# A norm's reciprocal root in two GpSimd steps, a divided output one round later, and nine shared SBUF buffers in a two-layer cross-attention kernel

## The chip, the cores and the metric

The kernel runs on one core of a Trainium2 chip. The engines are named as in the profile: PE is TensorE (PEld its weight loads), DVE is VectorE, ACT is ScalarE, POOL is GpSimd, and SP issues the DMAs. The metric is the device time of one execution in microseconds (us); smaller is better. The kernel before was timed in three runs: 3214.34, 3212.0 and 3215.55 us, with 3214.34 as their median.

## The reference

Two layers of the same block work on `x` of shape (4, 512, 320), with a context of shape (4, 1601, 192), all in float32. Each block has self attention with 20 heads of 16 columns, cross attention over the 1601 context rows, and a gated feed-forward part:

```
h1 = _ln(x, n1_g, n1_b)
x = _attn(h1, h1, q1, k1, v1, o1_w, o1_b, heads) + x
h2 = _ln(x, n2_g, n2_b)
x = _attn(h2, context, q2, k2, v2, o2_w, o2_b, heads) + x
h3 = _ln(x, n3_g, n3_b)
proj = h3 @ ff_w1 + ff_b1
a, g = jnp.split(proj, 2, axis=-1)
ff = a * jax.nn.gelu(g, approximate=False) @ ff_w2 + ff_b2
return ff + x
```

`_ln` subtracts a row's mean and multiplies by `rsqrt(v + EPS)`, then by a gain, and adds a bias. That reciprocal root is the first thing that the change touches. `_attn` takes a softmax over the keys.

## The kernel before, in words

**Units and chunks.** The program is a list of units that are emitted in order. A unit of attention is one batch row and one group of four heads, so there are 20 units of self attention and 20 of cross attention in each layer. A unit of the feed-forward part is one batch row. `main` works through a unit in chunks of 128 keys: 4 in a self unit, 13 in a cross unit. For each chunk PE computes the scores of four heads, keys along partitions, into PSUM tiles `st` (line 1062). ACT takes the exponentials into SBUF tiles `pr` (line 1068). One chunk later PE multiplies them with the values into a PSUM tile `av` (line 1082). PE also computes, among the scores, the scores `sps` of the next unit in the other orientation (line 891), from which DVE takes the row maxima (line 907).

**How `av` leaves PSUM.** The first chunk of a unit is copied by ACT to the unit's sum `o` (line 1093). Each later one is copied by ACT to a tile `vo` (line 1098) and added to `o` by GpSimd (line 1099). In the last unit of an attention stage DVE adds from PSUM instead (line 1095). `st` and `av` share one PSUM pool of four banks, so the scores of the next chunk need banks that ACT has read: those of the exponentials and that of `vo`.

**The pool `prs`.** The exponentials, the copied outputs `vo` and, in the feed-forward part, the gelu tiles `gl` share one SBUF pool with tag `pr` and eight buffers. When the four exponentials of a chunk are written, the four of the chunk before are still unread. That is eight. The fourth exponential of a chunk therefore gets the buffer that held `vo` of the chunk before, and ACT waits there for GpSimd's addition. In the program as built 574 exponentials carry such a wait for GpSimd, and no copy to `vo` does.

**The rest of GpSimd's queue.** Each engine runs its instructions in the order of the program. GpSimd also spreads projected queries and keys into slots of 32 rows (line 635: 0.48 to 0.56 us each by the profile's groups, eight for a self unit's queries and keys), adds a bias row to `x` (line 502), and takes the norm's root.

**The norm.** `add_norm` puts a norm's steps in a chain: statistics of four tiles of 128 rows (DVE, lines 464 and 465), `root`, the normalised rows `hn` (DVE, line 476), and transposes on PE (line 489). `root` calls `inverse_root`: three small DVE instructions make a first guess by integer arithmetic (lines 431 to 435), then one instruction scales and three Newton steps of four instructions each follow on GpSimd (lines 437 to 443), 13 in a row. `hn` may be emitted four rounds after `root`. A round is a tick of the planner's clock: a chunk of attention has two.

**The planner.** `steps` is called once a chunk, and runs pending pieces from the chains by their due times. `main` ticks the clock between the two halves of a chunk, and `steps` ticks it again. `LIGHT` pieces are limited to one or two a call. In `ff_main` the calls come at other intervals, and a pair of hidden blocks has four.

**A finished unit.** `add_finish` notes the round in `when`. `sums` (DVE transpose of `o`, line 979, and a reciprocal) may run two rounds later, then `divide`, then `turn`, whose four DMAs put the output into `aT`. The projections `ops` (line 1009) follow once five groups are there.

**The blank.** `blank`, a tile of 128 by 128, holds ones in the rows that carry the maximum and zeros elsewhere. DMAs copy it into the key buffers `kbuf` (line 138), whose last 128 columns begin at `4 * QT`.

Of the kernel before, what the change touches and what calls it, by code (L numbers as in the profile page):

```python
# [9 lines left out]
F32 = mybir.dt.float32  # L10
I32 = mybir.dt.int32
AF = mybir.ActivationFunctionType
ALU = mybir.AluOpType
# [9 lines left out]
P = 128  # L23
# [17 lines left out]
QT = (NC2 - 1) * 32  # L41
# [25 lines left out]
def kernel(ctx: ExitStack, tc: tile.TileContext, x, context, ws, out):  # L67
# [18 lines left out]
    nc = tc.nc  # L86
# [4 lines left out]
    one = ctx.enter_context(tc.tile_pool(name="one", bufs=1))  # L91
    two = ctx.enter_context(tc.tile_pool(name="two", bufs=2))
    three = ctx.enter_context(tc.tile_pool(name="three", bufs=3))
    prs = ctx.enter_context(tc.tile_pool(name="prs", bufs=8))
    dram = ctx.enter_context(tc.tile_pool(name="dram", bufs=1, space=bass.MemoryType.DRAM))
    ps_st = ctx.enter_context(tc.tile_pool(name="ps_st", bufs=4, space=PSUM))
    ps_m = ctx.enter_context(tc.tile_pool(name="ps_m", bufs=2, space=PSUM))
# [30 lines left out]
    nc.vector.memset(fill, 1.0)  # L128


    blank = const.tile([P, P], F32, name="blank")

    def blanks(k):

# [59 lines left out]
    def now(fs):  # L194
        for f in fs:
            f()
# [134 lines left out]
    LIGHT = 0.01  # L331
# [20 lines left out]
    def add(chain, cost, f, due, ready=yes, soon=yes):  # L352
        chains[chain].append((cost if isinstance(cost, tuple) else (cost,), due, ready, soon, f))
# [71 lines left out]
            assert chains[name], name  # L425
            run(name)

    def inverse_root(var):

        a, h, y, z = (two.tile([P, NQ], F32, tag=f"root{i}", name=f"root{i}") for i in range(4))  # L430
        nc.vector.tensor_scalar(a, var, EPS, None, ALU.add)  # L431
        nc.vector.tensor_scalar(
            z.bitcast(I32), a.bitcast(I32), 1, None, ALU.logical_shift_right
        )
        nc.vector.tensor_scalar(y.bitcast(I32), z.bitcast(I32), -1, 0x5F3759DF, ALU.mult, ALU.add)
        eng = nc.vector if start["on"] else nc.gpsimd
        eng.tensor_scalar(h, a, -0.5, None, ALU.mult)  # L437
        for _ in range(3):

            eng.tensor_tensor(z, y, y, ALU.mult)  # L440
            eng.tensor_tensor(z, z, h, ALU.mult)
            eng.tensor_scalar(z, z, 1.5, None, ALU.add)
            eng.tensor_tensor(y, y, z, ALU.mult)
        return y

    hn_used = []

# [7 lines left out]
    def add_norm(l, b, i, put, done, due):  # L455
        xb = xs[b]
        s = {}

        def stats(t):
            if t == 0:  # L460
                hn_used.append(b)
                s["mv"] = two.tile([P, NQ, 2], F32, tag="mv", name="mv")
            st = three.tile([P, 6], F32, tag="st6", name="st6")
            nc.vector.bn_stats(st, xb[:, t, :])
            nc.vector.bn_aggr(s["mv"][:, t, :], st)

        def root():
            s["rstd"] = inverse_root(s["mv"][:, :, 1])
            s["round"] = clock["round"]

        def normalise(t):
            if t == 0:
                s["hn"] = one.tile([P, NQ, D + REST], F32, tag="hn", name="hn")

            for to, at, n in ((0, 0, D), (D, D - REST, REST))[: 1 + i // 2]:
                nc.vector.tensor_scalar(  # L476
                    s["hn"][:, t, to : to + n], xb[:, t, at : at + n],
                    s["mv"][:, t, 0:1], s["rstd"][:, t : t + 1], ALU.subtract, ALU.mult,
                )
            s["round"] = clock["round"]  # L480

        def turn(k, at, n):
            if k == 0:
                s["hT"] = two.tile([P, 3, N], F32, tag="hT", name="hT")
                readers.append(done)
            ps = step_bank([P, N], "hps")
            n += REST if n == REST else 0
            for t in range(NQ):
                nc.tensor.transpose(ps[:n, t * P : (t + 1) * P], s["hn"][:, t, at : at + n], ident)  # L489
            if start["on"] and k == 1:  # L490
                nc.vector.tensor_scalar(
                    s["hT"][:n, k, :], ps[:n, :],
                    lng[i][:n, k : k + 1], lnb[i][:n, k : k + 1], ALU.mult, ALU.add,
                )
            else:
                nc.scalar.activation(
                    s["hT"][:n, k, :], ps[:n, :], AF.Identity,
                    bias=lnb[i][:n, k : k + 1], scale=lng[i][:n, k : k + 1],
                )
            for t in ((0,), (1,), (2, 3))[k]:  # L500

                nc.gpsimd.tensor_tensor(xb[:, t, :], xb[:, t, :], brow[(3 * l + i) % 2], ALU.add)  # L502
            if k == 2:
                hn_used.pop()
                put(s["hT"])

        for t in range(NQ):
            add(
                "norm", LIGHT, lambda t=t: stats(t), due - 22 + t,
                (lambda: stage[b] == 3 * l + i and not hn_used and b in loaded) if t == 0 else yes,  # L510
                (lambda: b == 0 or clock["round"] >= loaded[b] + 5) if t == 0 else yes,
            )
        add("norm", LIGHT, root, due - 18)
        for t in range(NQ):
            add(
                "norm", LIGHT, lambda t=t: normalise(t), due - 13 + t, yes,
                (lambda: clock["round"] >= s["round"] + 4) if t == 0 else yes,
            )
        for k, at, n in (DK if i < 2 else FK + [(2, 2 * P, REST)]):
            add(  # L520
                "norm", 0.58, lambda k=k, at=at, n=n: turn(k, at, n), due - 6 + 2 * k,
                may_overwrite if k == 0 else yes, lambda: clock["round"] >= s["round"] + 1,
            )
# [443 lines left out]
    def add_finish(u):  # L967

        when = [clock["round"]]

        def since(i, n):
            return lambda: len(when) > i and clock["round"] >= when[i] + n

        turned = two.tile([P, N // SLOT, SLOT], F32, tag="oturn", name="oturn")

        def sums():
            nc.vector.transpose(turned.rearrange("p b s -> p (b s)"), u.o)
            u.rd = two.tile([P, N // SLOT], F32, tag="rd", name="rd")  # L980
            nc.vector.reciprocal(u.rd, turned[:, :, DH])
            when.append(clock["round"])

        def divide():
            nc.vector.tensor_tensor(
                turned[:, :, :DH], turned[:, :, :DH],
                u.rd.rearrange("p (b o) -> p b o", o=1).to_broadcast([P, N // SLOT, DH]), ALU.mult,
            )
            nc.vector.transpose(u.o, turned.rearrange("p b s -> p (b s)"))
            when.append(clock["round"])  # L990

        def turn():

            if u.g == 0:
                held["outT"] = two.tile([P, 3, N], F32, tag="aT", name="aT")
            for j in range(HG):
                f = u.g * GD + j * DH
                k = next(k for k, at, n in DK if at <= f < at + n)
                row = f - DK[k][1]
                dma(out=held["outT"][row : row + DH, k, :], in_=u.o[j * SLOT : j * SLOT + DH, :])  # L1000
            if u.g == G - 1:
                end(held["outT"])

        def project(aT, t, part):
            cols = slice(part * D // 2, (part + 1) * D // 2)
            ps = step_bank([P, 512], "ops")
            for k, at, n in DK:
                for f, m in tiles_of(P):
                    nc.tensor.matmul(  # L1009
                        ps[f : f + m, : D // 2],  # L1010
                        lhsT=aT[:n, k, t * P + f : t * P + f + m],
                        rhs=wo[:n, k, cols],
                        start=(k == 0),
                        stop=(k == 2),
                    )
            nc.vector.tensor_tensor(xs[u.b][:, t, cols], ps[:, : D // 2], xs[u.b][:, t, cols], ALU.add)

        def end(aT):
            now = clock["round"]
            held["open"] += 1  # L1020
            for t in range(NQ):
                for part in range(2):
                    add(
                        "project", (0.317,) * 3, lambda t=t, part=part: project(aT, t, part),
                        now + 6 + u.nch * t + u.nch // 2 * part, yes, lambda: clock["round"] >= now + 3,
                    )
            add("project", 0.0, done, now + 6 + u.nch * NQ)

        def done():
            held["open"] -= 1  # L1030
            after(u)

        r = when[0]
        add("divide", LIGHT, sums, r - 20, yes, since(0, 2))
        add("divide", LIGHT, divide, r - 20, yes, since(1, 1))

        add("divide", 0.0, turn, r - 20, lambda: u.g or held["open"] < 2, since(2, 1))
# [325 lines left out]
    max_reduce(first)  # L1363
    max_end(first)
    now(load_x(1))
    now(blanks(kbuf[0][:, 4 * QT :]))
    loads.extend(load_x(2))
    for k in kbuf[1:]:
        loads.extend(blanks(k))
# [54 lines left out]
```

## Time and profile before

| what | value |
|---|---|
| runs | 3214.34, 3212.0, 3215.55 us; median 3214.34 us |
| the profiled execution | 3212.79 us, with a span of 3211.0 us and a mean granted TensorE clock of 0.999 |
| busy, share of the span | PE 99%, PEld 46%, DVE 64%, ACT 61%, POOL 37% |
| additions `o<-o,vo` on POOL (L1099) | 576, 736.2 us in all, 1278 ns each |
| exponentials on ACT (L1068) | 2720, 1412.7 us in all, 601 ns each |
| maxima on DVE (L907) | 974 and 339, about 1.2 us each |
| root on POOL (L437 and L440 to L443) | 23 roots of 13 instructions, 0.20 to 0.23 us each |

The span is the time from the first to the last recorded instruction. In a timeline a line begins with the start, in us from the span's start, and the duration in us; `xN` at the end means N instructions merged, and square brackets give the engine's idle time before the line and who ended it. A matmul of 32-bit numbers is recorded as two instructions, so one chunk's `av`, four matmuls, shows as x8.

### The profile page before, as it was taken

What the parts mean: (1) busy time and instruction counts of PE and PEld (TensorE: products, weight loads), DVE (VectorE), ACT (ScalarE), POOL (GpSimd) and SP (SyncE); (2) the same over time, 40 slices, a digit from 0 to 9 for tenths busy, and PEclk for the clock granted to TensorE, in tenths of its full rate; (3) what the DMA queues carried; (4) which work ended last, traced back from release to release, by engine and by line L of the source; (5) the groups of instructions that cost most, each with busy time, mean ns of one, the idle gap of its engine ahead of it and who ended that gap; (6) DMA issues with size and microseconds to landing.
All of it is one profiled execution on the core that took longest, in us unless ns stands there. A gap on an engine that the chain in (4) does not pass through costs nothing.

```text
span 3211.0 us, 81827 instructions
## 1 busy us (share of the span) xinstructions
PE 3170.7 (99%) x33970; PEld 1465.7 (46%) x33970; DVE 2062.9 (64%) x2663; ACT 1966.1 (61%) x3951; POOL 1203.1 (37%) x1617
## 2 busy tenths in 40 slices
PE   9999999999999999999999999999999999999999
PEld 3444444444444444354444444444444444443555
DVE  7776877778778677422247778777777777773221
ACT  4666577777777777611146665777778777785110
POOL 4555234444443443211225553344444444442000
PEclk9999999999999999999999999999999999999999
DMA  2130011100100100100012100010010010001000
GB/s 67 48 78 17 14 24 40 33 21 19 33 21 20 31 16 11 39 6 0 1 30 56 38 14 14 21 29 16 16 31 11 16 33 10 15 10 37 9 11 15
DMA packets 104999, 77.94 MB, mean 24 GB/s; under 512 B 42924, under 2 KB 95156, under 8 KB 104628
## 3 DMA queue, kind: packets, MB, share of 16 engines
q1 hardware_dynamic: 104544, 72.70, 9.3%
q8 instruction: 268, 4.39, 0.6%
q14 instruction: 103, 0.84, 0.1%
q0 software_dynamic: 64, 0.00, 0.0%
q10 hardware_dynamic: 20, 0.00, 0.0%
HBM read 33.04 MB, written 7.93 MB: 13 GB/s over the span
## 4 chain that ended last, share of the span: by engine, by line
PE 63%; DVE 2%; POOL 1%; ACT 0%; issue 0%; DMA 0%; SPq 0%; POOLq 0%; DVEq 0%
PE st L1062 15%; PE av L1082 13%; PE fps L1182 9%; PE sps L891 8%; PE yps L1221 5%; PE fps L1194 2%; PE ops L1009 2%; PE kps L743 2%; PE qps L687 2%; PE vps L836 2%; PE sps L915 1%; PE vps L818 1%; PE kps L713 1%; PE hps L489 1%; DVE nmax L907 1%; DVE pm L907 1%
## 5 line engine op out<-in xcount | busy, mean ns | idle before, releaser
L1068 ACT ACTIVATE pr<-st 128x512 f32<-128x512 f32 (+1 forms) x2720 | 1412.7, 601 | 432.1 <-PE sps L891 349.0
L1062 PE MATMUL st<-q,kT 32*128 32x512 f32 (+1 forms) x5440 | 1374.4, 615 | 9.7 <-ACT pr L1068 5.7
L907 DVE TENSOR_REDUCE pm<-sps 128x2 f32<-128x1024 f32 (+1 forms) x974 | 1134.8, 1203 | 271.9 <-PE sps L891 265.8
L891 PE MATMUL sps<-kT,q 32*128 32x512 f32 x5120 | 1272.6, 620 | 14.3 <-DVE nmax L907 11.7
L1099 POOL TENSOR_TENSOR o<-o,vo 128x512 f32<-128x512 f32 x576 | 736.2, 1278 | 1389.0 <-ACT vo L1098 1248.3
L1062 PEld LDWEIGHTS st<-q,kT 32*128 32x128 f32 (+1 forms) x5440 | 511.3, 181 | 528.0 <-ACT pr L1068 309.3
L1082 PE MATMUL av<-pr,vals 128*32 128x512 f32 (+1 forms) x5440 | 730.4, 605 | 0.2
L907 DVE TENSOR_REDUCE nmax<-sps 128x2 f32<-128x1024 f32 (+1 forms) x339 | 378.4, 1157 | 155.9 <-PE sps L891 152.8
L891 PEld LDWEIGHTS sps<-kT,q 32*128 32x128 f32 x5120 | 408.5, 183 | 120.7 <-issue 79.3
L1098 ACT COPY vo<-av 128x512 f32<-128x512 f32 x576 | 347.4, 603 | 41.8 <-PE av L1082 37.8
L1082 PEld LDWEIGHTS av<-pr,vals 128*32 128x32 f32 (+1 forms) x5440 | 109.9, 108 | 495.3 <-ACT pr L1068 483.5
L1182 PE MATMUL fps<-hT,w 128*128 128x512 f32 x640 | 288.2, 599 | 1.1 <-DVE hid L1201 0.6
L1200 ACT ACTIVATE gl<-fps,b 128x512 f32<-128x512 f32 x80 | 50.7, 684 | 387.4 <-PE fps L1194 387.3
L635 POOL TENSOR_SCALAR q<-qst,keep,zero 64x128 f32<-64x128 f32 (+1 forms) x476 | 230.4, 484 | 48.6 <-ACT qst L699 15.4
L1182 PEld LDWEIGHTS fps<-hT,w 128*128 128x128 f32 x640 | 117.3, 190 | 148.6 <-issue 143.2
L1201 DVE SCALAR_TENSOR_TENSOR hid<-fps,b,gl 128x512 f32<-128x512 f32 x48 | 33.8, 746 | 163.1 <-ACT gl L1200 163.1
L1009 PEld LDWEIGHTS ops<-wo,aT 112*32 112x32 f32 (+1 forms) x3072 | 97.7, 110 | 68.4 <-issue 37.6
L687 PE MATMUL qps<-hT,wq 112*32 112x128 f32 (+3 forms) x2880 | 125.6, 308 | 0.5 <-DVE pm L907 0.5
L1009 PE MATMUL ops<-wo,aT 112*32 112x160 f32 (+1 forms) x3072 | 125.2, 300 | 0.2
L687 PEld LDWEIGHTS qps<-hT,wq 112*32 112x32 f32 (+1 forms) x2880 | 86.2, 110 | 79.0 <-issue 38.0
L437 POOL TENSOR_SCALAR root<-root 128x4 f32<-128x4 f32 x23 | 5.3, 230 | 309.4 <-DVE root L431 308.8
L502 POOL TENSOR_TENSOR x<-x,brow 128x320 f32<-128x320 f32 x96 | 84.0, 893 | 89.1 <-DVE hn L476 78.3
(88 smaller groups left out, 2182.4 us busy)
## 6 DMA issues: line engine op xcount, KB each, us to landing
kT<-kst SPq DMA_DIRECT2D x320, 48.0 KB
aT<-o SPq DMA_DIRECT2D x320, 32.0 KB
q<-turned SPq DMA_DIRECT2D x636, 1.0 KB
w<-in_L_xattn_ff_w_dram SPq DMA_DIRECT2D x20, 256.0 KB
ctxT<-ctxT SPq DMA_DIRECT2D x24, 208.0 KB
ctxT<-ctxT SPq DMA_DIRECT2D x12, 416.0 KB
ctxin<-in_ctx_dram SPq DMA_DIRECT2D x24, 192.0 KB
w<-in_L_xattn_ff_w_dram SPq DMA_DIRECT2D x20, 160.0 KB
```

Source lines behind the costliest of these rows:

```text
L635: nc.gpsimd.tensor_scalar(to, stage[rows, :w], keep[b][rows], more[rows], ALU.mult, ALU.add)
L687: nc.tensor.matmul(ps[to, :w], lhsT=wq[:n, k, gs], rhs=first.hT[:n, k, at[i] : at[i] + w], start=(k == 0), stop=(k == 2),)
L891: nc.tensor.matmul(ps, lhsT=u.q[j * SLOT : (j + 1) * SLOT, t * P : (t + 1) * P], rhs=u.kT[j * SLOT : (j + 1) * SLOT, u.k0 + s * 512 : u.k0 ...
L907: nc.vector.tensor_reduce(to[:, j : j + n], part, AX.X, ALU.max, negate=(ns == 1))
L1009: nc.tensor.matmul(ps[f : f + m, : D // 2], lhsT=aT[:n, k, t * P + f : t * P + f + m], rhs=wo[:n, k, cols], start=(k == 0), stop=(k == 2),)
L1062: nc.tensor.matmul(st[:r, :], lhsT=u.kT[rows, u.k0 + u.cols[c] : u.k0 + u.cols[c] + r], rhs=u.q[rows, :], start=True, stop=True)
L1068: nc.scalar.activation(p[:r], st[:r], AF.Exp)
L1082: nc.tensor.matmul(ps[i * SLOT : (i + 1) * SLOT, :], lhsT=columns_of[:r, head : head + SLOT], rhs=pr.pop((c, j))[:r, :], start=True, stop= ...
L1098: nc.scalar.copy(vo, ps)
L1099: nc.gpsimd.tensor_tensor(u.o, u.o, vo, ALU.add)
L1182: nc.tensor.matmul(ps, lhsT=w1[:, k, i * FF + c * P : i * FF + (c + 1) * P], rhs=u.hT[:, k, :], start=(k == 0), stop=False,)
L1221: nc.tensor.matmul(ps[:, :D], lhsT=hid[c][:, t * P : (t + 1) * P], rhs=w2[:, c, :], start=(c == 0), stop=(c == NHC - 1),)
```

## The change

It does four things. The 13 instructions of the root become two pieces of the chain: the scaling and one Newton step, then, in a later call of the planner, the other two steps; `hn` may follow one round after the second piece, where it was four after the whole. The first piece of a finished unit's output, `sums`, becomes eligible three rounds after the unit's end, where it was two. The pool `prs` gets nine buffers. The tile `blank` goes: the last 128 columns of the first key buffer take its place, and the DMA that filled them is not issued.

```diff
-    prs = ctx.enter_context(tc.tile_pool(name="prs", bufs=8))
+    prs = ctx.enter_context(tc.tile_pool(name="prs", bufs=9))
...
-    blank = const.tile([P, P], F32, name="blank")
+    blank = kbuf[0][:, 4 * QT :]
...
-    def inverse_root(var):
+    def guess_root(var):
...
         eng.tensor_scalar(h, a, -0.5, None, ALU.mult)
-        for _ in range(3):
-
-            eng.tensor_tensor(z, y, y, ALU.mult)
-            eng.tensor_tensor(z, z, h, ALU.mult)
-            eng.tensor_scalar(z, z, 1.5, None, ALU.add)
-            eng.tensor_tensor(y, y, z, ALU.mult)
-        return y
+        return h, y, z
+
+    def better_root(h, y, z):
+        eng = nc.vector if start["on"] else nc.gpsimd
+        eng.tensor_tensor(z, y, y, ALU.mult)
+        eng.tensor_tensor(z, z, h, ALU.mult)
+        eng.tensor_scalar(z, z, 1.5, None, ALU.add)
+        eng.tensor_tensor(y, y, z, ALU.mult)
...
-        def root():
-            s["rstd"] = inverse_root(s["mv"][:, :, 1])
+        def root(step):
+            if step == 0:
+                s["root"] = guess_root(s["mv"][:, :, 1])
+                s["rstd"] = s["root"][1]
+            for _ in range(step + 1):
+                better_root(*s["root"])
             s["round"] = clock["round"]
...
-        add("norm", LIGHT, root, due - 18)
+        for step in range(2):
+            add(
+                "norm", 0.0 if step else LIGHT, lambda step=step: root(step), due - 18 + step, yes,
+                (lambda: clock["round"] > s["round"]) if step else yes,
+            )
         for t in range(NQ):
             add(
                 "norm", LIGHT, lambda t=t: normalise(t), due - 13 + t, yes,
-                (lambda: clock["round"] >= s["round"] + 4) if t == 0 else yes,
+                (lambda: clock["round"] >= s["round"] + 1) if t == 0 else yes,
             )
...
-        add("divide", LIGHT, sums, r - 20, yes, since(0, 2))
+        add("divide", LIGHT, sums, r - 20, yes, since(0, 3))
...
-    now(blanks(kbuf[0][:, 4 * QT :]))
```

## The prediction

> **What bounds the kernel now.** I read the page first, then the waits by pair of engines, then the timeline around the 23 roots.
>
> ```profile
> PE 3170.7 (99%) x33970; PEld 1465.7 (46%) x33970; DVE 2062.9 (64%) x2663; ACT 1966.1 (61%) x3951; POOL 1203.1 (37%) x1617
> ```
>
> PE is busy nearly throughout, with a mean granted clock of 0.999, so nothing on another engine matters unless it stops PE. Does GpSimd, where the change works, stop it? Its rows of waits (who waited for whom: us in total, times, longest):
>
> ```profile
> ACT pr L1068 <- POOL o L1099: 24.0, 27, 2.9
> DVE oturn L979 <- POOL o L1099: 13.4, 5, 5.8
> ```
>
> ACT waits 24.0 us for GpSimd's additions, because the fourth exponential takes the buffer of the last `vo`. What that costs PE is read from the time between one chunk's `av` and the next. A self unit's root:
>
> ```profile
> 125.71 1.07 PE L1082 MATMUL av<-pr,vals 128*32 128x512 f32 x8
> 125.94 2.48 POOL L635 TENSOR_SCALAR kT<-kst,keep,ones 64x256 f32<-64x256 f32 x4
> 126.87 0.62 ACT L1098 COPY vo<-av 128x512 f32<-128x512 f32 x1
> 128.50 0.23 POOL L437 TENSOR_SCALAR root<-root 128x4 f32<-128x4 f32 x1
> 128.85 1.57 ACT L1068 ACTIVATE pr<-st 128x512 f32<-128x512 f32 x3 [0.70 <-PE sps L891]
> 129.62 1.07 PE L1082 MATMUL av<-pr,vals 128*32 128x512 f32 x8
> 131.88 0.20 POOL L443 TENSOR_TENSOR root<-root,root 128x4 f32<-128x4 f32 x1
> 132.03 1.26 POOL L1099 TENSOR_TENSOR o<-o,vo 128x512 f32<-128x512 f32 x1
> 133.33 0.60 ACT L1068 ACTIVATE pr<-st 128x512 f32<-128x512 f32 x1 [2.91 <-POOL o L1099]
> 133.98 0.93 PE L1062 MATMUL st<-q,kT 32*128 32x512 f32 x1 [1.26 <-ACT pr L1068]
> 134.25 0.37 DVE L476 TENSOR_SCALAR hn<-x,mv,root 128x320 f32<-128x320 f32 x1
> 137.62 1.09 PE L1082 MATMUL av<-pr,vals 128*32 128x512 f32 x8
> ```
>
> `vo` is ready at 127.49, but its addition stands behind slots and the whole root and runs at 132.03. Three exponentials run, the fourth waits 2.91 us, and PE's scores wait for its bank. The chunk takes 137.62 - 129.62 = 8.00 us; the one before, with the same work, took 129.62 - 125.71 = 3.91. It loses 4.09. Three other self roots show the same: 221.24 to 227.93 (6.69), 1735.10 to 1741.47 and 1824.68 to 1831.05 (6.37 each); they lose 2.78, 2.46 and 2.46. The four lose **11.8 us**.
>
> A cross unit's root costs less:
>
> ```profile
> 1023.13 0.23 POOL L437 TENSOR_SCALAR root<-root 128x4 f32<-128x4 f32 x1
> 1025.89 1.07 PE L1082 MATMUL av<-pr,vals 128*32 128x512 f32 x8
> 1026.66 1.26 POOL L1099 TENSOR_TENSOR o<-o,vo 128x512 f32<-128x512 f32 x1
> 1027.90 0.42 DVE L476 TENSOR_SCALAR hn<-x,mv,root 128x320 f32<-128x320 f32 x1
> 1027.96 0.59 ACT L1068 ACTIVATE pr<-st 65x512 f32<-65x512 f32 x1 [1.33 <-POOL o L1099]
> 1030.24 1.06 PE L1082 MATMUL av<-pr,vals 65*32 65x512 f32 x8
> ```
>
> 4.35 us against 2.92 of an undisturbed chunk (1005.81 to 1008.73): 1.43 lost. The six cross roots, near 552, 788, 1028, 2154, 2390 and 2623, lose 0.95, 0.59, 1.43, 0.97, 1.13 and 0.91, **6.0 us**. So the roots cost PE 17.8 us. Two more chunks with an ACT wait of 0.82 but no root, at 1252.27 and 2614.57, take 4.32 and 4.33 where others of their work have a median of 3.57: 1.5 us.
>
> **How much of that can be had: a rule against the busy row.** The engine's idle time would say far less: before the late scores of the self roots PE is idle 1.26, 0.87, 1.25 and 1.25 us, before two of the cross ones 0.58 and 0.37, some 5.6 in all. The Trainium skill (Trainium Kernel Development and Optimization, Performance Expectations) says that matmul busy time is a bad measure of how near a kernel is to its limit, because matmuls are pipelined. The intervals are on its side here, so I take them: by the idle row the roots would be worth 5.6 us, by the intervals 17.8.
>
> **The change part by part.**
>
> *Root in two pieces.* The 13 GpSimd instructions stay and still take 3.58 us (128.50 to 132.08, 0.275 each). In the program's order the pieces are 5 and 8 instructions, 1.4 and 2.2 us, and in twelve attention roots one `o<-o,vo` now stands between them. At 128.50 the first piece ends at 129.9 and the addition at 131.2, not 133.3. The fourth exponential wanted it at 130.42.
>
> *Nine buffers.* As built, 496 copies to `vo` and 78 exponentials now wait for GpSimd, where 574 exponentials did. The wait moves one ACT instruction on, about 0.5 us (1027.96 to the copy at 1028.45). In the self roots, where the next chunk's `av` is copied to `o`, it moves past that copy. With the addition at 131.2, nothing is left to wait for. I count all 11.8 us as gained. For the two chunks without a root I take 1.0 of the 1.5, since 0.5 of the 0.82 is covered.
>
> In a cross root the addition also comes in time: at 1023.13 the first piece ends at 1024.5, `vo` is there at 1024.73, and the addition ends at 1026.1, before the copy wants its buffer at about 1027.1. ACT's wait goes. **What is late next is `hn`**, which keeps its place among DVE's reductions while the second piece ends later: 1026.1 + 2.2 = 1028.3, and DVE reaches `hn` at 1027.90. By the same sum the six cross `hn` wait 0.2, 0, 0.4, 0.2, 0.8 and 0.8 us: 2.4. Queued behind are the reductions of L907, two a chunk, 2.36 of 2.92 us, and PE waits for their banks, so I charge them one to one. In the self roots `hn` waits about 1.1 us (second piece to 133.4, `hn` wanted at 132.3), but there the next reduction's scores come later and the two `sps` tiles cover it: 0, or 4.4 without the cover.
>
> *A rule against this change.* Behind the second piece the next addition starts at once, beside `hn`. The trace has such pairs:
>
> ```profile
> 546.07 1.27 POOL L1099 TENSOR_TENSOR o<-o,vo 128x512 f32<-128x512 f32 x1 [0.26 <-ACT vo L1098]
> 546.49 0.87 DVE L431 TENSOR_SCALAR root<-mv 128x4 f32<-128x4 f32 x1
> ...
> 139.50 1.27 POOL L1099 TENSOR_TENSOR o<-o,vo 128x512 f32<-128x512 f32 x1 [6.21 <-ACT vo L1098]
> 140.01 0.94 DVE L476 TENSOR_SCALAR hn<-x,mv,root 128x320 f32<-128x320 f32 x1
> ```
>
> L431, 0.165 us at the median, took 0.87 and ended with the addition; `hn` took 0.94, not 0.37, and ended 0.18 after one. The Trainium skill (SBUF — State Buffer, SBUF: two separate sides) calls the ports that DVE and GpSimd share an exclusive lock, held for the whole instruction. Then an `hn` released by the second piece waits out the next addition, 1.27 + 0.18 = 1.45 us, wherever `vo` is already there: in three of the cross roots (1028, 2390, 2623), by the times of ACT's copies. Without the lock the cross roots would cost 2.4 and gain 6.0 - 2.4 = 3.6; with it they cost 2.4 + 3 x 1.45 = 6.8, a loss of 0.8. The rows show the lock, so I take the loss of 0.8. Bounds: +3.6 and, if all six meet an addition, -5.1.
>
> *Outputs one round later.* A chunk has two rounds, the unit's end is noted at round R, and the planner is called at R+1 and R+3. Two rounds or three, `sums` runs at R+3. In attention DVE's order is unchanged. Only in the feed-forward part do pieces move: `ops` come a block or two later, `hn` up to two rounds earlier, the transposes with it. PE's instructions are the same in number. In that part DVE is busy 27 us of 100 and POOL 13 (1430 to 1530), and before the change `hn` came 3.7 to 26.7 us after the root's end, so a root ends before its nearer `hn` or keeps only an idle DVE waiting. 0, bounds -2 and +2; the cover is DVE's 5 to 8 us of idle time before each pair of gated blocks, and without it an `hn` there would cost its own 0.4 to 1.0 us. The two roots just before that part (1312 and 2906) find GpSimd empty and run through. The four DMAs of `turn` and all others keep their order on SP.
>
> *The blank.* One DMA issue less at the start (about 0.6 us of SP, which PE doesn't wait for), and three GpSimd instructions write another tile: 0, bounds -0.5 and +0.5.
>
> **The sum.** 11.8 + 1.0 - 0.8 = 12.0 us. The profiled execution, 3212.8 us with 1.8 around its span, would take 3200.8; it lay 1.5 under the median of the runs shown, so the forecast is **3202 us**. A measurement can tell about 0.2%, 6.4 us, from no change.
>
> **The rivals.**
>
> *A, as above,* with the cross roots anywhere within their bounds: 3197 to 3207.5. Chance 0.79, likeliest 3202.
>
> *B, the gain is PE's idle time, or the wait only moves.* For: the busy row, and the wait on `vo` holds the fourth bank just as the exponential's did. Against: the 8.00 us interval, and additions that end 2.1 us earlier. 5.6 us: 3208.7, within 0.2%. Also here: two of the four parts being without effect (the later output is, in attention) and the rest half of what I count. Chance 0.13.
>
> *C, slower: `hn` becomes DVE's stop.* Twelve attention roots have an addition between their pieces, and that addition waits for ACT's copy. If each `hn` keeps the reductions, and so PE, waiting w, the change costs 12w - 18.8 against the losses named. It breaks even at w = 1.6 and is slower by over 0.2% from w = 2.1; at 2.3 it takes 3223. For: 1.8 is what I count in the worst two cross roots (0.8, then 1.0 to 1.45 for the lock). Against: the self roots have no further `vo` waiting. Chance 0.08.
>
> Range 3194 (no lock, 3.6 gained, and +4 from smaller ACT waits and the feed-forward part) to 3213 (B with the lock met in all six cross roots, 5.1 instead of 0.8: 4.3 more). Faster 0.79, same 0.13, slower 0.08.
>
> **What would show it.** Right: no chunk of a self unit at 8.00 or 6.37 us; ACT's waits for POOL under 6 us in all; the DVE wait of `oturn` for POOL smaller; a new row of DVE `hn` waiting for POOL `root`, 3 to 8 us, and `hn` above 1.2 us in a few cross units. Wrong: self chunks near 6 us with ACT waiting in `vo` instead; cross chunks over 4.5 us behind `hn`; or feed-forward stretches that differ by over 3 us.

## The result and the profile after

The changed kernel takes 3204.78 us (median of 7 runs, 3203.94 to 3208.95), the kernel before 3214.34 (7 runs, 3212.0 to 3217.19): a ratio of 0.9973, 95% interval 0.9963 to 0.9982. By the ratio it is 0.27% faster (the medians differ by 9.6 us). The forecast was 3202 with a range of 3194 to 3213. The profiled execution has a span of 3202.9 us where before had 3211.0.

All times below compare *stretches*: from the `av` with which a root's chunk begins to the `av` four chunks later, so that what a root gives back in the next chunks is in the number. The line numbers of the changed kernel are 12 higher: the addition `o<-o,vo` is L1111, the copy to `vo` L1110, `av` L1094, `hn` L484, the root L438 to L448.

The busy row of the page, and rows of waits (who waited for whom: us in total, times, longest):

```profile
PE 3167.7 (99%) x33970; PEld 1462.6 (46%) x33970; DVE 2068.9 (65%) x2663; ACT 1972.4 (62%) x3951; POOL 1202.3 (38%) x1617
```

```profile
DVE hn L484 <- POOL root L448: 15.3, 10, 3.5
DVE oturn L991 <- POOL o L1111: 5.8, 1, 5.8
```

PE's busy time fell by 3.0 us where the span fell by 8.1: the busy row hides most of it. The row of ACT's exponentials waiting for the addition, 24.0 us before, is gone, `oturn` waits 5.8 us instead of 13.4, and a new row stands there, `hn` waiting for the root. Of its 15.3 us only 5.2 belong to attention roots; 10.1 are three waits in the feed-forward parts (at 1420, 1491 and 3009), where PE has no idle time of over 0.15 us for 10 us behind them. The self root, in the timeline of the changed kernel:

```profile
128.59 1.07 PE L1094 MATMUL av<-pr,vals 128*32 128x512 f32 x8
128.65 1.28 POOL L1111 TENSOR_TENSOR o<-o,vo 128x512 f32<-128x512 f32 x1
129.89 0.20 POOL L445 TENSOR_TENSOR root<-root 128x4 f32<-128x4 f32 x1
131.78 2.06 ACT L1080 ACTIVATE pr<-st 128x512 f32<-128x512 f32 x4 [0.76 <-PE sps L903]
132.15 0.45 DVE L484 TENSOR_SCALAR hn<-x,mv,root 128x320 f32<-128x320 f32 x1 [0.96 <-POOL root L448]
132.50 1.06 PE L1094 MATMUL av<-pr,vals 128*32 128x512 f32 x8
134.41 1.27 POOL L1111 TENSOR_TENSOR o<-o,vo 128x512 f32<-128x512 f32 x1 [2.29 <-ACT vo L1110]
134.89 1.07 DVE L997 TENSOR_TENSOR oturn<-oturn,rd 128x256 f32<-128x256 f32 x1
136.08 1.07 PE L1094 MATMUL av<-pr,vals 128*32 128x512 f32 x8
```

The addition stands between the two pieces, four exponentials run as one group, and the chunk takes 132.50 - 128.59 = 3.91 us, not 8.00. But `hn` waits 0.96, `oturn`'s product stands beside the next addition (1.07; its mean over the kernel is 0.61), and the next chunk takes 136.08 - 132.50 = 3.58 where it took 2.95. The cross root near 1020:

```profile
1018.61 0.23 POOL L438 TENSOR_SCALAR root<-root 128x4 f32<-128x4 f32 x1
1020.36 1.27 POOL L1111 TENSOR_TENSOR o<-o,vo 128x512 f32<-128x512 f32 x1 [0.47 <-ACT vo L1110]
1021.43 1.06 PE L1094 MATMUL av<-pr,vals 128*32 128x512 f32 x8
1023.61 0.20 POOL L448 TENSOR_TENSOR root<-root,root 128x4 f32<-128x4 f32 x1
1023.75 1.27 POOL L1111 TENSOR_TENSOR o<-o,vo 128x512 f32<-128x512 f32 x1
1023.84 1.37 DVE L484 TENSOR_SCALAR hn<-x,mv,root 128x320 f32<-128x320 f32 x1 [0.38 <-POOL root L448]
1024.67 1.06 PE L1094 MATMUL av<-pr,vals 65*32 65x512 f32 x8
1025.13 2.34 DVE L919 TENSOR_REDUCE pm<-sps 128x2 f32<-128x1024 f32 x2
1028.58 1.07 PE L1094 MATMUL av<-pr,vals 128*32 128x512 f32 x8
```

The root's chunk falls from 4.35 to 3.24 us (1021.43 to 1024.67). Then `hn` waits 0.38, the next addition starts in the moment of its release, `hn` takes 1.37 us and ends with it, the two reductions stand behind, and the next chunk takes 3.91 us where it took 2.92. So the root's chunk gains 1.11 and the one behind it loses 0.98; a further 0.48 goes in the third.

### The profile page after: what moved, and what is told of

Same layout as the page of the kernel before. It is cut to its first block, busy times and chain, and to the rows that moved or that the text cites. A ratio compares the mean times of both kernels' runs of the same rounds, so it can differ in the third digit from the quotient of the medians.

```text
span 3202.9 us, 81370 instructions
## 1 busy us (share of the span) xinstructions
PE 3167.7 (99%) x33970; PEld 1462.6 (46%) x33970; DVE 2068.9 (65%) x2663; ACT 1972.4 (62%) x3951; POOL 1202.3 (38%) x1617
## 5 line engine op out<-in xcount | busy, mean ns | idle before, releaser
L1111 POOL TENSOR_TENSOR o<-o,vo 128x512 f32<-128x512 f32 x576 | 734.3, 1275 | 1373.1 <-ACT vo L1110 1201.8
L1074 PEld LDWEIGHTS st<-q,kT 32*128 32x128 f32 (+1 forms) x5440 | 504.0, 181 | 520.0 <-ACT pr L1080 291.7
L1094 PE MATMUL av<-pr,vals 128*32 128x512 f32 (+1 forms) x5440 | 729.3, 605 | 0.2
L1110 ACT COPY vo<-av 128x512 f32<-128x512 f32 x576 | 339.7, 590 | 45.5 <-PE av L1094 41.4
L1094 PEld LDWEIGHTS av<-pr,vals 128*32 128x32 f32 (+1 forms) x5440 | 110.0, 108 | 493.3 <-ACT pr L1080 480.1
L438 POOL TENSOR_SCALAR root<-root 128x4 f32<-128x4 f32 x23 | 5.3, 231 | 332.7 <-DVE root L432 332.2
L1240 DVE TENSOR_TENSOR x<-yps,x 128x320 f32<-128x320 f32 x32 | 15.7, 491 | 146.5 <-PE yps L1233 146.5
```

The costliest lines, as they stand in the source:

```text
L1074: nc.tensor.matmul(st[:r, :], lhsT=u.kT[rows, u.k0 + u.cols[c] : u.k0 + u.cols[c] + r], rhs=u.q[rows, :], start=True, stop=True)
L1094: nc.tensor.matmul(ps[i * SLOT : (i + 1) * SLOT, :], lhsT=columns_of[:r, head : head + SLOT], rhs=pr.pop((c, j))[:r, :], start=True, stop= ...
L1110: nc.scalar.copy(vo, ps)
L1111: nc.gpsimd.tensor_tensor(u.o, u.o, vo, ALU.add)
```

## The experiments

My theory T was that the root's addition held a buffer too long, and that what the change gives back is `hn`, waiting for the second piece and then meeting an addition of GpSimd, which holds it up at ports that the two share. The rivals: only one of the two parts works; the loss is DVE's load or other moved work; the meeting is not real. The table has the profiled execution of each kernel: the four self stretches, the six cross stretches (the last one is six chunks long and takes in one of the two chunks without a root), and all else, in us against before; and how often the granted clock fell to half in that execution before the kernel's end (in each of the two marked rows one of these drops lasted twice as long as the others).

| kernel | median us | ratio (95%) | self | cross | else | drops |
|---|---|---|---|---|---|---|
| before | 3214.34 | | 0 | 0 | 0 | 2 |
| the change | 3204.78 | 0.9973 (0.9963 to 0.9982) | -9.9 | +2.5 | -0.7 | 1 |
| nine buffers alone | 3202.33 | 0.9954 (0.9941 to 0.9966) | -7.1 | -3.0 | +0.4 | 1 |
| two pieces, eight buffers | 3205.97 | 0.9963 (0.9949 to 0.9976) | -10.6 | +2.9 | +0.9 | 2 |
| later outputs alone | 3215.45 | 0.9998 (0.999 to 1.0006) | +2.0 | 0.0 | +0.5 | 3 |
| `hn` one chunk later | 3202.07 | 0.9949 (0.9936 to 0.9961) | -12.8 | -3.2 | +2.6 | 1 |
| two pieces in self units only | 3200.62 | 0.9944 (0.9932 to 0.9957) | -9.8 | -2.8 | -1.0 | 1 |
| the same, `hn` later there | 3193.97 | 0.9927 (0.9915 to 0.994) | -12.7 | -2.7 | -3.3 | 1 |
| one Newton step more | 3224.61 | 1.0022 (1.0014 to 1.0031) | -5.9 | +15.6 | +3.5 | 5* |
| root on DVE | 3217.98 | 1.0001 (0.9993 to 1.001) | -9.3 | +8.7 | +11.4 | 4* |
| Newton steps two and one | 3201.99 | 0.9964 (0.995 to 0.9977) | -9.8 | +0.2 | -2.3 | 0 |

Each ratio is against runs of before on the same chip (medians of 3214.0 to 3217.0), so ratios, not medians, are to be compared between them. Neither is free of the clock: the runs of before differ among themselves by their drops (last section), and a ratio takes these in. The three columns are single executions, and add up to the difference of the spans.

**Nine buffers alone.** On the kernel before:

```diff
-    prs = ctx.enter_context(tc.tile_pool(name="prs", bufs=8))
+    prs = ctx.enter_context(tc.tile_pool(name="prs", bufs=9))
...
-    blank = const.tile([P, P], F32, name="blank")
+    blank = kbuf[0][:, 4 * QT :]
...
-    now(blanks(kbuf[0][:, 4 * QT :]))
```

The blank goes with the buffer, as in the change; it was not tried by itself.

> The kernel before with only the ninth buffer for exponentials and copied outputs (and, to make room for it, the blank in the key buffer as in the change). The root stays in one piece, so no `hn` waits for it. Theory T (the late addition holds a buffer, and with nine the wait stands one ACT instruction on, past the copy to `o` in a self unit): the four self roots keep at most 0.7 us of their wait, so most of the 11.8 us comes back; the cross roots' wait shrinks by 0.5 us each, worth 2 to 3: 3200 to 3204 us, faster than the change itself, which pays for `hn`. Rival 1 (the root in two pieces did it: the addition still ends at 133.3 and ACT's wait only moves from the exponential to the copy to `vo`): 2.4 us of wait left at each self root, the cross roots as before: 3209 to 3214.

Measured: 3202.33 us, T's side. The first self root:

```profile
131.27 0.62 ACT L1093 COPY o<-av 128x512 f32<-128x512 f32 x1
132.44 1.27 POOL L1099 TENSOR_TENSOR o<-o,vo 128x512 f32<-128x512 f32 x1
133.74 2.06 ACT L1068 ACTIVATE pr<-st 128x512 f32<-128x512 f32 x4 [1.20 <-POOL o L1099]
133.74 0.71 DVE L979 STREAM_TRANSPOSE oturn<-o 128x512 f32<-128x512 f32 x1 [1.94 <-POOL o L1099]
135.06 2.32 DVE L907 TENSOR_REDUCE nmax<-sps 128x2 f32<-128x1024 f32 x2
```

The root is whole and the addition as late as ever. ACT still waits, 1.20 us where it was 2.91 and T allowed 0.7; the chunk takes 4.28. What T had left out is `oturn`, which needs the same addition and makes the reductions late: the next chunk takes 4.10 and not 2.95. That is why the self stretches gain 7.1 and not nearly 11.8. In the cross units there is nothing to give back, and the stretches gain 3.0 where the change loses 2.5.

**The root in two pieces with eight buffers.** The changed kernel with

```diff
-    prs = ctx.enter_context(tc.tile_pool(name="prs", bufs=9))
+    prs = ctx.enter_context(tc.tile_pool(name="prs", bufs=8))
...
-        add("divide", LIGHT, sums, r - 20, yes, since(0, 3))
+        add("divide", LIGHT, sums, r - 20, yes, since(0, 2))
```

> The changed kernel with eight buffers, as before, and the outputs not one round later: the root in two pieces and the blank remain. Theory T: the addition of the first self root ends at about 131.2 where the fourth exponential wanted its buffer at 130.42, so ACT waits 0.8 us and not 2.91; the four self chunks take 4 to 4.6 us, 10 to 11.8 us back; the cross roots pay for `hn` as in the change, and the 0.5 us that the ninth buffer gave elsewhere is gone: 3205 to 3208 us. Rival 2 (the ninth buffer did it): self chunks near 6 us, cross chunks dearer by `hn`: 3213 to 3217.

Measured: 3205.97 us, as T has it; self roots -10.6. Its waits:

```profile
DVE hn L484 <- POOL root L448: 19.1, 11, 3.5
ACT pr L1080 <- POOL o L1111: 9.1, 21, 0.8
```

The longest wait of an exponential is 0.8 us, the 0.8 of the expectation. So either part alone gets most of the self roots, and the two do not add. Of the change's parts, the ninth buffer is the one that gains without a price; beside the two pieces it brings only the two chunks without a root (0.0 here, 0.5 us each with nine).

**Outputs one round later alone.** On the kernel before:

```diff
-        add("divide", LIGHT, sums, r - 20, yes, since(0, 2))
+        add("divide", LIGHT, sums, r - 20, yes, since(0, 3))
```

> The kernel before with only the outputs turned one round later. All theories: the order of DVE's work changes only in the feed-forward part, where DVE has idle time: within 2 us of before, 3212 to 3216. If the later output were worth something by itself (a rival for a part of the gain): below 3210.

Measured: 3215.45 us, ratio 0.9998: no effect. Of its +2.0 in the self stretches 1.6 stand in the one where the clock dropped (last section).

**`hn` one chunk later.** The changed kernel with

```diff
-                (lambda: clock["round"] >= s["round"] + 1) if t == 0 else yes,
+                (lambda: clock["round"] >= s["round"] + 3) if t == 0 else yes,
```

> The changed kernel with the first `hn` allowed three rounds after the second piece of the root and not one, so one chunk later. Theory T (what the change gives back in the chunks after a root is `hn` that waits for the second piece and then stands beside an addition): the rows of `hn` waiting for the root in attention vanish, the give-back of about 0.65 us at each self root and 1 to 1.5 at the cross roots returns in part: 3199 to 3202. Rival (the give-back is the addition and `hn` meeting at the shared ports wherever `hn` stands, or DVE's load itself): 3203 to 3206, no better than the change, with other `hn` of over 1.2 us.

Measured: 3202.07 us, just over T's range. There is no row of `hn` waiting for the root any more, and the self stretches gain 12.8 instead of 9.9: 2.9 us had been given back there. But with `hn` go the transposes, and PE's work is dealt out otherwise over the chunks between the roots; one such stretch lost 3.4 us and another gained 1.4, so for the cross units this run doesn't decide.

**Two pieces in self units only.** The changed kernel with

```diff
+        split = i != 1 or b == 0
+        wait = 4 if not split else 1
...
-            for _ in range(step + 1):
+            for _ in range(step + 1 if split else 3):
...
-        for step in range(2):
+        for step in range(2 if split else 1):
...
-                (lambda: clock["round"] >= s["round"] + 1) if t == 0 else yes,
+                (lambda: clock["round"] >= s["round"] + wait) if t == 0 else yes,
```

> The changed kernel, but the root of the norms that run beside cross units (second norm of a layer, batches 1 to 3) stays in one piece; in self units and in the feed-forward part it keeps two. The orders of PE and DVE are those of the change; only GpSimd's differs, at the cross roots. Theory T (the nine buffers alone serve the cross roots, and the two pieces only make `hn` late there): the six cross roots go from the 2.9 us that the change lost there against before to the 2.5 us that the nine buffers alone gained, so 5.4 us less than the change: 3198 to 3200 us, and no `hn` of over 1.2 us in the cross units. Rival (the loss at the cross roots comes from other things that the change moves, the ninth buffer's copies among them): 3203 to 3206, as the change.

Measured: 3200.62 us, 0.6 over T's range by the median; the cross stretches go from +2.5 to -2.8, 5.2 us, for 5.4 expected. DVE and ACT execute the same lists as in the change, and PE the same instructions; only GpSimd's order at the cross roots differs. The root near 1017:

```profile
1019.53 1.06 PE L1096 MATMUL av<-pr,vals 128*32 128x512 f32 x8
1020.24 1.27 POOL L1113 TENSOR_TENSOR o<-o,vo 128x512 f32<-128x512 f32 x1
1021.48 0.42 DVE L486 TENSOR_SCALAR hn<-x,mv,root 128x320 f32<-128x320 f32 x1
1021.54 0.59 ACT L1112 COPY vo<-av 128x512 f32<-128x512 f32 x1 [0.79 <-POOL o L1113]
1023.34 1.07 PE L1096 MATMUL av<-pr,vals 65*32 65x512 f32 x8
```

ACT waits 0.79 us again and the root's chunk takes 3.81, but `hn` runs at once in 0.42, and the chunk behind it takes 2.92. So in a cross unit the two pieces are a loss once there are nine buffers.

**The same with `hn` one chunk later in self units.** The kernel just described with

```diff
-        wait = 4 if not split else 1
+        wait = 4 if not split else 1 if i == 2 else 3
```

> As the kernel with two pieces in self units only, and there the first `hn` is allowed one chunk later. Theory T (in self units, too, what is given back is the wait of `hn`): the four self roots gain 12.8 us as they did with the later `hn` everywhere, not 9.9, and the cross roots 2.5: 3195 to 3198 us. Rival (the later `hn` meets other work): 3198 to 3201.

Measured: 3193.97 us, ratio 0.9927, faster than T's range and the fastest kernel of this study, 0.46% below the change by the ratios, 0.34% by the medians. The self stretches gain 12.7, as foreseen. Another 2.3 us come from the chunks behind the first feed-forward part, where the later `hn` also moved PE's work; I had not foreseen that.

**One Newton step more in the second piece.** The changed kernel, its second piece 12 instructions long and not 8:

```diff
-            for _ in range(step + 1):
+            for _ in range(2 * step + 1):
```

> The changed kernel with one more Newton step in the second piece of the root (12 instructions and not 8, 3.3 us and not 2.2). Theory T (in attention, PE pays for every us that the second piece ends later, through `hn` and the reductions behind it): 1.1 us more at most of the ten attention roots: 3211 to 3216 us, and the longest intervals stand in the chunk after each root. Rival (the wait of `hn` is covered, and only the meeting with the next addition at the shared ports costs): the addition moves with the root, `hn` meets it as before: 3204 to 3207.

Measured: 3224.61 us, dearer than T's 3211 to 3216. Against the change, the self stretches lose 0.93, 1.17, 0.93 and 0.95 and three of the cross ones 1.08, 1.15 and 1.17: the 1.1 us of the dose, one to one. The other three lose 2.73, 2.71 and 4.33, and in each of these the clock fell to half after the stall. One of them in the timeline:

```profile
2396.96 1.27 POOL L1111 TENSOR_TENSOR o<-o,vo 128x512 f32<-128x512 f32 x1
2397.04 1.72 DVE L484 TENSOR_SCALAR hn<-x,mv,root 128x320 f32<-128x320 f32 x2 [1.85 <-POOL root L448]
2398.68 2.34 DVE L919 TENSOR_REDUCE pm<-sps 128x2 f32<-128x1024 f32 x2
2399.95 3.80 PE L755 MATMUL kps<-ctxT,w 32*64 32x224 f32 x92 [1.90 <-DVE pm L919]
```

The wait of `hn` (1.85), its meeting with the addition, the reductions behind it, PE's stop of 1.90: the whole chain of the theory in four lines. The rival, that the wait is covered, is out. T's error was mostly the clock: four more drops than in the change's profile, some 1.5 us each, and one of the five twice as long.

**The root on DVE.** The changed kernel with

```diff
-        eng = nc.vector if start["on"] else nc.gpsimd
+        eng = nc.vector
```

in both functions.

> The changed kernel with the whole root on DVE: GpSimd has no root any more, `hn` waits for nobody, and DVE gets 13 instructions of about 0.165 us, 2.1 us a root, in two pieces of 0.8 and 1.3 us. Theory T (DVE is the engine that a cross unit can't spare: two reductions take 2.36 of a chunk's 2.92 us): the waits and meetings of `hn` go, 5.4 us at the cross roots, and DVE's lumps cost up to 1.5 us at each of them; in self units 0 to 1: 3203 to 3211 us. Rival (two `sps` tiles cover such lumps): 3196 to 3200.

Measured: 3217.98 us, no faster than before. The rival (such lumps are covered) is out, and T was too low. The cross stretches lose 6.2 us more than in the change, although `hn` waits for nobody, and the chunk before five of the six loses 0.3 to 1.4 us more, 4.1 in all: there the first piece now stands on DVE. T had also left out the two roots at 257 and 1858, where the first cross units are prepared (1.5 us each). And it had the meetings gone, but the root's own operations meet additions now:

```profile
1027.10 1.29 POOL L1111 TENSOR_TENSOR o<-o,vo 128x512 f32<-128x512 f32 x1 [1.92 <-ACT vo L1110]
1027.30 1.12 DVE L446 TENSOR_TENSOR root<-root,root 128x4 f32<-128x4 f32 x1
```

Twelve of them take 0.9 to 1.3 us where 0.16 is normal, three in the change. The profile has three more drops of the clock than the change's, but it is the slowest execution of the 13, 5.6 us above their median; the others ran at a mean clock of 0.999 or 1.000, so the drops are no reason for the median. The price of the change is thus smaller than that of giving DVE the root.

**The Newton steps divided two and one.** The changed kernel with the addition behind two steps:

```diff
-            for _ in range(step + 1):
+            for _ in range(2 - step):
```

> The changed kernel with the Newton steps divided the other way: two in the first piece (9 instructions, 2.5 us), one in the second (4, 1.1 us). The orders of PE and DVE are those of the change. Theory T (the wait of `hn` for the second piece, and what meets it then, is what the change gives back): the second piece ends 1.1 us earlier after the addition and the addition 1.1 us later. The cross `hn` have no wait left (0.8 at most in the change's sum, less 1.1), so the cross roots go from 2.9 us lost to a gain of 1 to 2.5; in the self roots the addition at about 132.3 is late by 0.4 to 0.8 for the copy, which costs about what `hn` gives back: 3199 to 3202 us. Rival (`hn` meets an addition anyway, because the addition now stands 1.1 us later and beside it): the cross roots as in the change, 3203 to 3207.

Measured: 3201.99 us, inside T's range, but by luck: 2.3 us come from outside the stretches, and the trace is half the rival's. The six cross stretches go from +2.5 to +0.2, 2.2 us better, not to -1 or -2.5:

```profile
1021.23 0.20 POOL L448 TENSOR_TENSOR root<-root,root 128x4 f32<-128x4 f32 x1
1021.42 1.27 POOL L1111 TENSOR_TENSOR o<-o,vo 128x512 f32<-128x512 f32 x1
1021.52 1.35 DVE L484 TENSOR_SCALAR hn<-x,mv,root 128x320 f32<-128x320 f32 x1
1022.79 2.34 DVE L919 TENSOR_REDUCE pm<-sps 128x2 f32<-128x1024 f32 x2
```

`hn` waits for the root no more, and still takes 1.35 us, because it meets the addition. The self stretches stay at -9.8: there the later addition takes what `hn` no longer waits for (DVE waits 0.85 us for it before `oturn`). So of the 5.2 us that the two pieces cost in the cross units, 2.2 were the wait. The other 3.0 stay, and go by the trace to the meeting (at five of the six roots an `hn` takes 1.35 to 1.47 us), less what the root's chunk gains beyond the ninth buffer's share; no run takes the meeting away alone.

**The ports by themselves.** Behind the whole work of the kernel before, DVE runs three forms, first alone and then beside GpSimd. `hns` are operations of the form of `hn` (128x320), `tiny` some of the root's (128x4), and `reds` reductions of a PSUM tile of 128x1024; GpSimd adds tiles of 128x512:

```diff
+    hns(8)
+    tiny(4)
+    reds(4)
...
+    for _ in range(24):
+        nc.gpsimd.tensor_tensor(mo, mo, mv_, ALU.add)
...
+    hns(8)
+    tiny(4)
+    reds(6)
```

> The kernel before with a block behind its work that measures DVE beside GpSimd: on DVE eight operations of the form of `hn` (128x320, two scalars a partition), four of the form of the root's (128x4) and four reductions of a 128x1024 PSUM tile, alone; then the same (six reductions) while GpSimd runs 24 additions of the form of the `o` addition (128x512, 1.27 us) back to back. Lock theory: alone 0.37, 0.165 and 1.17 us; beside the additions an `hn` starts only when an addition ends, so each takes 1.3 to 1.5 us (or the addition waits for it in turn), a root's operation up to 1.3, and the reductions, which read PSUM, stay at 1.17. Rival (the long `hn` of 1.37 us came from something else, such as the wait for the root's semaphore counted as work): all three keep their lengths beside the additions.

```profile
3212.52 3.69 DVE L1413 TENSOR_SCALAR q<-kT,ma 128x320 f32<-128x320 f32 x8
3216.12 0.78 DVE L1417 TENSOR_SCALAR mb<-ma 128x4 f32<-128x4 f32 x4
3216.81 4.99 DVE L1421 TENSOR_REDUCE mg<-mp 128x2 f32<-128x1024 f32 x4
3222.16 32.09 POOL L1429 TENSOR_TENSOR kT<-kT,kT 128x512 f32<-128x512 f32 x24
3223.48 10.84 DVE L1413 TENSOR_SCALAR q<-kT,ma 128x320 f32<-128x320 f32 x8
3234.23 2.82 DVE L1417 TENSOR_SCALAR mb<-ma 128x4 f32<-128x4 f32 x4
3236.96 7.51 DVE L1421 TENSOR_REDUCE mg<-mp 128x2 f32<-128x1024 f32 x6
```

The eight `hn` take 3.69 us alone and 10.84 beside the additions, 0.46 and 1.35 each: one to an addition. The four small ones take 0.78 and 2.82; two of them wait. (With the block the kernel takes 3257.06 us in its one run.) The reductions take 4.99 / 4 and 7.51 / 6 = 1.25 us each both times: they don't notice GpSimd. Whether that is their source in PSUM or the operation itself, this run doesn't separate. The additions keep their 1.26. The Trainium skill (SBUF — State Buffer, SBUF: two separate sides) calls the shared ports an exclusive lock, held for the whole instruction by a GpSimd operation or by a DVE operation of certain kinds, and the rows agree with that: an `hn` beside an addition costs 0.9 us more, though the reductions, which are most of DVE's work, do not pay.

## Why the prediction came out as it did

The direction, the mechanism and the range held: the addition leaves earlier, ACT's wait goes, and `hn` is late next. The profiled execution gained 8.1 us where the sum said 12.0, and two terms were mis-sized.

*Self roots, 11.8 counted, 9.9 measured.* The four root chunks gave back exactly that: 4.10 + 2.78 + 2.47 + 2.46 = 11.8. The term that was off is "0, or 4.4 without the cover" for the wait of `hn`: the wait is 0.96 us in three of the four and 0.58 in the fourth, the `sps` tiles don't cover it, and 0.87 us is lost in each of three stretches and 0.25 in the fourth: with the later `hn` they gain 12.7 and 12.8. The sum counted this gain for both parts together; two pieces alone gain 10.6, nine buffers alone 7.1.

*Cross roots, 0.8 lost by the sum, about 3.0 measured* (2.5 with a chunk that has no root). The root chunks gained 5.5 of the 6.0. The waits of `hn`, 2.4 by the sum, are 0.38, 0.69 and 0.69 in the trace and next to nothing in the other three, 1.9 in all; the division two and one makes them worth 2.2. What was mis-sized is the meeting: "in three of the cross roots", at 1.45 each. It takes place in all six: `hn` of 1.33 to 1.44 us where 0.42 is normal, 5.8 us together. In the three that were not named, the addition met the first `hn` at 783 and the second one at 545 and 2146; the sum had looked at the first alone and at its release. By these terms the six lose 5.8 + 2.2 - 5.5 = 2.5 us, near what the stretches show.

*Chunks without a root, 1.0 counted:* 4.32 to 3.79 and 4.34 to 3.79, 1.1, with nine buffers only. Right.

*Feed-forward part, 0 counted:* 0.9 us gained in the first one and 0.75 in a chunk behind it. Inside the ±2, but the prediction named no cause for a gain. It goes with the earlier `hn` and not with the two pieces: the kernel with `hn` one chunk later has the pieces too and gains neither, nor do nine buffers or the later output alone. Part of it is a stop of PE behind `hn` in the kernel before, which these three kernels keep and the change does not have:

```profile
1548.77 0.90 PE L489 MATMUL hps<-ident,hn 128*112 128x128 f32 x4 [0.72 <-DVE hn L476]
```

PE's idle time in the first feed-forward part falls by 0.4 us with it (4.55 to 4.17); the cause of the rest stays open.

*What was in no term:* the clock fell to half once in the change's profile, in a chunk at 798 that took 9.40 us and not 7.84. And two of the self roots' 4.09 and 2.78 contain such drops, before: the two roots without one lose 2.46. So the sum took for a wait what was partly the clock behind the wait; it came back all the same, because the stall went. An execution of before without these two drops would have had less to gain, about 1.5 us for each.

*The rivals.* B's 5.6 us of idle time: out, just by the interval of the ratio and clearly by 12.7 us in the self units. C's mechanism is real, at half its price: the ten attention roots inside stretches give back 2.9 + 8.0 us, 1.1 each, where C turns slower at 1.6. With one Newton step more it is 2.2, `hn` does become DVE's stop, and the kernel is slower than before: 3224.61 us, where C had 3223 for w = 2.3. That the two lie so close is luck, since drops of the clock, which C did not count, are a good part of it. (A's upper end, 3207.5, is more than its cross bounds give, 3202 + 4.3 = 3206.3; nothing rests on it.)

*The signs named beforehand.* No self chunk takes 8.00 or 6.37 us any more, and ACT waits 5.7 us for GpSimd in all. `hn` waits longer for the root than the 3 to 8 us foreseen, 15.3, because of the three waits in the feed-forward parts; 5.2 is the part in attention.

## What to carry to other kernels

When work is cut in two so that something else can come between, follow what waits for its end: here the addition came earlier and the normalisation later, and in the units where DVE is the tight engine the second cost more than the first brought. Try the extra buffer before the new order: it lets the wait pass without making anything late. And count, for each operation that is released at a moment when the neighbour engine starts too, what they share; a wait that just fits can still meet the next operation.

## What was not expected of the hardware

*Half clock behind short stalls.* The granted clock falls to half for some 3.4 us (twice for 6.8), now and then, after PE stood still for about a microsecond. The windows view (from:to, us of the window, busy of PE, PEld, DVE, ACT and POOL, the mean granted clock, then the share and GB/s of the DMA engines) of the change, and of before around its first self root:

```profile
800.00:805.00 5.00, 3.85 (x98) 2.93 (x98) 1.42 (x3) 0.03 (x1) 0.88 (x1) 0.72 0.10 23
805.00:810.00 5.00, 5.00 (x42) 2.65 (x44) 2.98 (x3) 4.16 (x9) 0.98 (x1) 0.94 0.27 72
```

```profile
130.00:135.00 5.00, 3.74 (x41) 1.81 (x37) 2.67 (x6) 2.09 (x5) 2.72 (x9) 0.93 0.35 104
135.00:140.00 5.00, 5.00 (x33) 1.83 (x31) 3.40 (x4) 2.62 (x6) 0.50 (x1) 0.73 0.02 3
```

Both pairs lack 1.7 us of clock, 5 x (0.28 + 0.06) and 5 x (0.07 + 0.27), which is half the clock for 3.4 us; the trace's own records of the clock have 0.5 for 3.41 us. PE is idle 1.55 us to 801.1 in the first and 1.26 us to 134.0 in the second. Each drop costs about 1.5 us (9.40 for 7.84 in the chunk at 798). In these profiles they followed stalls of 0.6 to 1.9 us, while others of the same lengths had none; later outputs alone had one at 1831 behind the stall where before had none. What decides is not shown. The drops also go with the differences between executions: of 23 runs of before on one chip, those with a mean clock of 0.999 took 3213.4 to 3214.1 us and those with 0.997 took 3218.5 to 3220.5. The Trainium skill (TensorE: Matmul & The Clock Gate, Why this matters for your kernels) says to leave no idle gaps of over some 3 us between bursts of matmuls; here, in a kernel that is 99% busy, much shorter ones were sometimes enough, so the page's figure doesn't hold as a limit. So a stall costs its own time, and sometimes 1.5 us more.

*Parts that do not add.* The spans fall by 9.7 us with the ninth buffer alone, by 6.8 with the two pieces alone and by 8.1 with both and the later output (by the ratios 0.46%, 0.37% and 0.27%, with intervals that overlap). Both remove the same wait, and only one of them has a price.
